# Start of a fused attention and bottleneck kernel: last input tile in four transfers, statistics chunk by chunk, weight sums between the group steps, and eight idle matrix products

## The chip, the cores and the metric

The kernel runs on one NeuronCore of a Trainium2 chip. The metric is the device time of one launch in microseconds (us). The kernel before takes 3301.49 us (median of 3 runs, 3300.69 to 3302.63).

## The reference, cut to what matters

For eight images of 512 channels and 64 x 64 pixels, float32, two residual layers are computed:

```python
x = x + deform_attention(_gn(x))     # layer 0
x = x + bottleneck(_gn(x))           # layer 1

def _gn(v, G=32, eps=1e-5):          # group norm, groups of 16 channels
    g = v.reshape(B_, G, C_ // G, H_, W_)
    m = jnp.mean(g, axis=(2, 3, 4), keepdims=True)
    s = jnp.var(g, axis=(2, 3, 4), keepdims=True)
    return ((g - m) / jnp.sqrt(s + eps)).reshape(v.shape)

q = jnp.einsum('oc,bchw->bohw', w_q, x)   # first step of layer 0, x is normed
```

The rest of layer 0 samples q at 256 learned points, projects keys and values from the samples, and attends from all 4096 pixels with 8 heads. Layer 1 is a narrow convolution stack. The change touches only the group norm of the first image and the first steps of its q projection.

## The kernel before, in words

**Tiling.** An image lies in SBUF as 128 partitions x 4 channel chunks x 4096 pixels. Pixels are cut into 8 tiles of 512. `x_tile(b, t)` is tile t of image b, 128 x 4 x 512, one megabyte. Two images have room at once.

**Order of the work.** Everything is placed by hand, in program order on each engine (`tc.manual_schedule()`, L1058). Generators yield between steps so that the main loop can interleave them. The program starts with image 0 alone:

1. SyncE's queue loads x of image 0 (`load_x(0)`, L1059, eight transfers, L196), then the q weights into `wbuf` (L1060, L135), then x of image 1, then the key and value weights and small ones.
2. `norm_x` (L198) runs one VectorE `bn_stats` for each tile and chunk, 32 in all (L201). `drain` at L1070 lets all of it be issued before anything else.
3. `norm_q` (L209) begins with `group_stats` (L164): four `bn_aggr` (L169), a small product `gps` that averages the means over the groups (L173), four small VectorE operations (L175 to L179), a second product `gpsb` for the variances (L182), and then `ve` (L184) and a power on GpSimd (L185) that gives one over the deviation. It yields after the aggregates, and again ahead of `gpsb`. Back in `norm_q` it yields once more, then normalises tile 1 on GpSimd and tile 0 on VectorE (L217), one chunk after the other, and makes `shift` (L230).
4. `make_q` (L1044, L1078) runs `project_q` (L233). It multiplies each tile by the q weights with seven half-size products in place of eight, in the manner of Strassen and Winograd. For that it needs four sums of quarters of the weights (`of_weights`, L248: s1, s2, a new w21, s4) and four of the quarters of each tile (`of_tile`, L261: t1, t2, a new x12, a new x21). In the loop at L340 to L342 they are issued in turn: s1, t1, s2, t2, w21, x12. s4 follows during tile 0 (L366). Products of tile 0 go p1 (w11, x11), p2 (w12, x21), p6 (s2, t2), p7 (w21, x12), p5 (s1, t1), p4 (w22, x21), p3 (s4, x22), all at L275. Each has four matmuls, and a float32 matmul appears as two matmul instructions in the profile, so that a product has eight.

For image 1 the weight sums are not made again; for later images they are made inside `project_q`, as for image 0.

Of the kernel before, what the change touches and what calls it, by code (L numbers as in the profile page):

```python
# [8 lines left out]
F32 = mybir.dt.float32  # L9
# [7 lines left out]
P = 128  # L17
B = 8
C = 512
NCC = C // P  # L20
HW = 64
N = HW * HW
TP = 512
NT = N // TP
# [25 lines left out]
def kernel(  # L50
# [15 lines left out]
    nc = tc.nc  # L66
    xs = x.rearrange("b (cc p) n -> b p cc n", p=P)
# [7 lines left out]
    ps_a = ctx.enter_context(tc.tile_pool(name="ps_a", bufs=1, space=PSUM))  # L75
# [6 lines left out]
    wbuf = cpool.tile([P, NCC, TP], F32, name="wbuf")  # L82
# [28 lines left out]
    ident = cpool.tile([P, P], F32, name="ident")  # L111
# [43 lines left out]
    def drain(*gens):  # L155
        for gen in gens:
            for _ in gen:
                pass
# [2 lines left out]
    def new_stats(which, b):  # L161
        return small.tile([P, NCC, NT, 6], F32, tag=f"st{which}", name=f"st{which}_{b}")

    def group_stats(st, which, b):  # L164

        nm = f"{which}_{b}"
        mv = small.tile([P, NCC, 2], F32, tag="mv", name=f"mv{nm}")
        for cc in range(NCC):
            nc.vector.bn_aggr(mv[:, cc, :], st[:, cc].rearrange("p t s -> p (t s)"))  # L169
        mean, var = mv[:, :, 0], mv[:, :, 1]  # L170
        yield None
        gps = ps_mm.tile([P, TP], F32, tag="mm", name=f"gps{nm}")
        nc.tensor.matmul(gps[:, :NCC], cst[:, K_GRP : K_GRP + P], mean, start=True, stop=True)  # L173
        gs = small.tile([P, 2, NCC], F32, tag=f"gs{which}", name=f"gs{nm}")
        nc.vector.tensor_copy(gs[:, 0], gps[:, :NCC])  # L175
        dv = small.tile([P, NCC], F32, tag="dv", name=f"dv{nm}")
        nc.vector.tensor_sub(dv, mean, gs[:, 0])
        nc.vector.tensor_mul(dv, dv, dv)
        nc.vector.tensor_add(dv, dv, var)  # L179
        yield None  # L180
        gps2 = ps_mm.tile([P, TP], F32, tag="mm", name=f"gpsb{nm}")
        nc.tensor.matmul(gps2[:, :NCC], cst[:, K_GRP : K_GRP + P], dv, start=True, stop=True)  # L182
        ve = small.tile([P, NCC], F32, tag="ve", name=f"ve{nm}")
        nc.vector.tensor_scalar_add(ve, gps2[:, :NCC], EPS)  # L184
        nc.gpsimd.tensor_tensor(gs[:, 1], ve, nhalf, ALU.pow)  # L185
        return gs
# [7 lines left out]
    def load_x(b, order=range(NT), queue=nc.sync):  # L194
        for t in order:
            queue.dma_start(x_tile(b, t), xs[place[b]][:, :, t * TP : (t + 1) * TP])  # L196

    def norm_x(b, st, order=range(NT)):  # L198
        for t in order:
            for cc in range(NCC):  # L200
                nc.vector.bn_stats(st[:, cc, t, :], x_tile(b, t)[:, cc, :])  # L201
                yield None

    def quarters(a):

        h = C // 2
        return [[a[:, 2 * i : 2 * i + 2, h * j : h * (j + 1)] for j in range(2)] for i in range(2)]

    def norm_q(b, st, norms):  # L209

        gs = yield from group_stats(st, 0, b)
        shift = small.tile([P, NCC], F32, tag="shift", name=f"shift_{b}")

        def normalise(t, cc):
            xc, scale = x_tile(b, t)[:, cc, :], gs[:, 1, cc : cc + 1]
            if t < 2:
                (nc.vector, nc.gpsimd)[t].tensor_scalar(  # L217
                    xc, xc, gs[:, 0, cc : cc + 1], scale, ALU.subtract, ALU.mult
                )
            else:  # L220
                nc.scalar.activation(
                    xc, xc, AF.Identity, bias=shift[:, cc : cc + 1], scale=scale
                )

        norms[b] = normalise
        yield None
        for t in (1, 0):
            for cc in range(NCC):
                normalise(t, cc)
        nc.vector.scalar_tensor_tensor(shift, gs[:, 0], -1.0, gs[:, 1], ALU.mult, ALU.mult)  # L230
        yield None

    def project_q(b, normalise, mq, qd, pools, sums, aside=None):  # L233


# [6 lines left out]
        s1, s2, s4, t1, t2_, first = sums  # L242
# [1 line left out]

        (w11, w21), (w12, w22) = quarters(wbuf)
        V = nc.vector

        def of_weights(n):  # L248

            if b == 1:  # L250
                return
            if n == 1:
                V.tensor_add(s1, w21, w22)
            elif n == 2:
                V.tensor_sub(s2, s1, w11)
            elif n == 3:
                V.tensor_sub(w21, w11, w21)
            else:
                V.tensor_sub(s4, w12, s2)

        def of_tile(t, n):  # L261
            (x11, x12), (x21, x22) = quarters(x_tile(b, t))
            if n == 1:
                V.tensor_sub(t1, x12, x11)
            elif n == 2:
                V.tensor_sub(t2_, x22, t1)
            elif n == 3:
                V.tensor_sub(x12, x22, x12)
            else:
                V.tensor_sub(x21, x21, t2_)  # L270

        def product(bank, w, xh):
            for o in range(2):
                for k in range(2):
                    nc.tensor.matmul(  # L275
                        bank[:, o * 2 * P : (o + 1) * 2 * P],
                        w[:, k, o * P : (o + 1) * P],
                        xh[:, k, :],
                        start=(k == 0),
                        stop=(k == 1),  # L280
                    )
            return bank.rearrange("p (o n) -> p o n", o=2)
# [28 lines left out]
        def two_banks(t, n):  # L311
            two = ps_s.tile([P, 2, TP], F32, tag="s", name=f"pq_{b}_{t}_{n}")
            return two[:, 0, :], two[:, 1, :]
# [24 lines left out]
            )  # L338

        for n in range(1, 4):  # L340
            of_weights(n)
            of_tile(0, n)  # L342
        for t in range(NT):
            (x11, x12), (x21, x22) = quarters(x_tile(b, t))
            (q11, q12), (q21, q22) = quarters(q_tile(b, t))

            def pixels(k):

                if t:
                    by_pixel(t - 1, k)  # L350
                if t + 2 < NT:
                    normalise(t + 2, k)

            bank1, bank2 = two_banks(t, 0)
            p1 = product(bank1, w11, x11)
            p2 = product(bank2, w12, x21)
            nc.scalar.copy(q11, p1)
            of_tile(t, 4)
            if t:
                activate(t - 1)  # L360
            yield 4
            p6 = product(one_bank(t, 1), s2, t2_)
            pixels(0)
            V.tensor_add(q12, q11, p6)
            V.tensor_add(q11, q11, p2)
            if t == 0:  # L366
                of_weights(4)
            yield 2.5
            bank1, bank2 = two_banks(t, 2)
            p7 = product(bank1, w21, x12)  # L370
            pixels(1)
            V.tensor_add(q22, q12, p7)
            if aside and t in (3, 4):
                largest(2, t - 3)
            yield 2.5
            p5 = product(one_bank(t, 3), s1, t1)
            pixels(2)
            V.tensor_add(q12, q12, p5)
            if t + 1 < NT:
                of_tile(t + 1, 1)  # L380
                of_tile(t + 1, 2)
            yield 2.5
            p4 = product(bank2, w22, x21)
            pixels(3)
            V.tensor_add(q21, q22, p4)
            V.tensor_add(q22, q22, p5)
            if t + 1 < NT:
                of_tile(t + 1, 3)
            yield 2.5
            p3 = product(one_bank(t, 4), s4, x22)  # L390
            V.tensor_add(q12, q12, p3)
            if t == 2 and aside:
                aside()
            elif t + 1 < NT:
                largest(t, 0)
                largest(t, 1)
            yield 2
# [171 lines left out]
    exps, sums = {}, {}  # L569
# [469 lines left out]
    norms = {}  # L1039
# [13 lines left out]
    def room_for_sums(tiles):  # L1053

        places = [tiles[i // 2][:, i % 2, :] for i in range(6)]
        return [p.rearrange("p (k o) -> p k o", k=2) for p in places[:5]] + places[5:]

    with tc.manual_schedule():  # L1058
        load_x(0)  # L1059
        load_wq()  # L1060
        load_x(1)

# [4 lines left out]
                nc.sync.dma_start(wkv[i][j], w[:, 2 * j : 2 * j + 2, i * C : (i + 1) * C])  # L1067
        load_weights_late()
        st = new_stats(0, 0)
        drain(norm_x(0, st))  # L1070

        shared = [wout[:, i, :].rearrange("p (k o) -> p k o", k=2) for i in range(3)]
        shared += [kt[:, 0:2, :], kt[:, 2:4, :], wout[:, 3, :]]
        drain(norm_q(0, st, norms))

        st = new_stats(0, 1)
        blocks, other = norm_x(1, st), norm_q(1, st, norms)
# [19 lines left out]
        for g in range(len(names) + LAG):  # L1097
            b, r = divmod(g, ROUNDS)
# [78 lines left out]
    with tc.If(large > 0):  # L1177
        with tc.For_i(0, B, 1) as i:
            b = "m"
# [95 lines left out]
```

## Time and profile before

| quantity | us |
|---|---|
| median of three runs | 3301.49 |
| lowest and highest run | 3300.69, 3302.63 |
| the profiled execution, its own time | 3300.22 |
| span of its trace | 3298.4 |
| time outside the span | 1.8 |
| first `bn_stats` of image 0 starts | 7.31 |
| first product of the q projection starts | 33.71 |

The trace runs from the first to the last instruction of the profiled execution. All later moments are counted in microseconds from the start of the span. A row of the timeline has the start, the length from the first start to the last end, the engine, the line, the operation, the tile written and the tile read, the shapes, the count, and in brackets the idle time of the engine before it with what ended it. PE is TensorE, PEld is its weight load, DVE is VectorE, POOL is GpSimd, ACT is ScalarE and SP is SyncE.

### The profile page before, as it was taken

What the parts mean: (1) busy time and instruction counts of PE and PEld (TensorE: products, weight loads), DVE (VectorE), ACT (ScalarE), POOL (GpSimd) and SP (SyncE); (2) the same over time, 40 slices, a digit from 0 to 9 for tenths busy, and PEclk for the clock granted to TensorE, in tenths of its full rate; (3) what the DMA queues carried; (4) which work ended last, traced back from release to release, by engine and by line L of the source; (5) the groups of instructions that cost most, each with busy time, mean ns of one, the idle gap of its engine ahead of it and who ended that gap; (6) DMA issues with size and microseconds to landing.
All of it is one profiled execution on the core that took longest, in us unless ns stands there. A gap on an engine that the chain in (4) does not pass through costs nothing.

```text
span 3298.4 us, 46059 instructions
## 1 busy us (share of the span) xinstructions
PE 3212.1 (97%) x18196; PEld 1532.3 (46%) x18196; DVE 2321.9 (70%) x3666; ACT 1187.9 (36%) x1641; POOL 606.2 (18%) x576
## 2 busy tenths in 40 slices
PE   6999999999999999999999999999999999999996
PEld 5884223258332583326732276332853338433222
DVE  7885765786757767587766876668766687756565
ACT  2343333344324433344333443335433344333420
POOL 1130300230402204022130312204021040310201
PEclk9999999999999999999999999999999999999996
DMA  7232222662327532284323833257232482322713
GB/s 275 77 99 73 81 69 87 202 134 78 116 77 224 122 90 91 96 224 113 111 85 132 197 91 105 79 188 171 71 97 89 179 179 65 122 71 71 135 38 131
DMA packets 293873, 390.61 MB, mean 118 GB/s; under 512 B 18320, under 2 KB 157840, under 8 KB 293648
## 3 DMA queue, kind: packets, MB, share of 16 engines
q1 hardware_dynamic: 240368, 261.72, 24.3%
q0 software_dynamic: 53280, 125.86, 17.3%
q8 instruction: 145, 2.38, 0.3%
q14 instruction: 80, 0.66, 0.1%
HBM read 193.52 MB, written 192.94 MB: 117 GB/s over the span
## 4 chain that ended last, share of the span: by engine, by line
PE 90%; DVE 6%; issue 2%; DMA 1%; SPq 0%; ACT 0%; POOL 0%; ACTq 0%; DVEq 0%; POOLq 0%
PE pp L666 25%; PE pq L275 24%; PE ps L579 13%; PE pa L597 12%; PE pqt L324 4%; PE pn L624 3%; PE py L749 2%; PE pk L532 2%; PE pv L559 2%; DVE rn L637 1%; PE po L892 1%; DVE st L201 1%; DMA rn<-rn 1%; DVE es L609 1%; DVE rb L650 1%
## 5 line engine op out<-in xcount | busy, mean ns | idle before, releaser
L666 PE MATMUL pp<-image,wout 128*64 128x512 f32 x3584 | 823.5, 602 | 4.9 <-DVE image L652 3.2
L587 ACT ACTIVATE es<-ps 128x1024 f32<-128x1024 f32 x512 | 505.3, 1023 | 289.3 <-PE ps L579 201.3
L666 PEld LDWEIGHTS pp<-image,wout 128*64 128x64 f32 x3584 | 238.0, 137 | 551.8 <-issue 465.5
L597 PE MATMUL pa<-es,vt 128*64 128x512 f32 x2048 | 488.3, 597 | 1.7 <-ACT es L587 1.7
L275 PE MATMUL pq<-image,wbuf 128*128 128x256 f32 x2048 | 476.2, 381 | 1.9 <-DVE image L217 1.9
L518 POOL DMA_INDIRECT g<-qd,row x256 | 274.2, 1071 | 1024.5 <-DVE row L474 842.1
L673 DVE SCALAR_TENSOR_TENSOR image<-pp,vec,image 128x512 f32<-128x512 f32 x224 | 166.8, 745 | 415.4 <-PE pp L666 383.1
L579 PE MATMUL ps<-image,kt 64*64 64x512 f32 x3584 | 442.6, 602 | 1.0
L275 PEld LDWEIGHTS pq<-image,wbuf 128*128 128x128 f32 x2048 | 381.8, 191 | 54.4 <-issue 5.0
L604 ACT COPY image<-pa 128x512 f32<-128x512 f32 x224 | 132.1, 590 | 683.7 <-PE pa L597 628.3
L609 DVE TENSOR_TENSOR es<-es,es 128x1024 f32<-128x1024 f32 x256 | 310.6, 1213 | 71.5 <-PE pa L597 71.4
L597 PEld LDWEIGHTS pa<-es,vt 128*64 128x64 f32 x2048 | 137.3, 136 | 298.0 <-issue 273.9
L579 PEld LDWEIGHTS ps<-image,kt 64*64 64x64 f32 x3584 | 115.5, 132 | 312.1 <-issue 184.6
L637 DVE RECIPROCAL rn<-pn 128x512 f32<-128x512 f32 x64 | 214.7, 3355 | 13.7 <-PE pn L624 6.9
L334 ACT COPY qr<-pqt 128x512 f32<-128x512 f32 x224 | 131.2, 586 | 237.2 <-PE pqt L324 222.2
L185 POOL TENSOR_TENSOR gs<-ve,nhalf 128x4 f32<-128x4 f32 x16 | 16.7, 1042 | 1063.3 <-DVE ve L184 1063.3
L650 DVE STREAM_SHUFFLE rb<-rn 128x512 f32<-128x512 f32 x256 | 187.4, 732 | 0.5 <-issue 0.4
L275 PE MATMUL pq<-es,es 128*128 128x256 f32 x768 | 181.5, 379 | 0.0
L944 POOL DMA_DIRECT2D out_dram<-part x126 | 138.0, 1324 | 161.0 <-ACT part L939 153.7
L201 DVE BATCH_NORM_STATS2 st<-image 128x6 f32<-128x512 f32 x256 | 158.6, 678 | 7.5 <-DMA image<-in_x_dram 7.4
L676 DVE BATCH_NORM_STATS2 st<-image 128x6 f32<-128x512 f32 x224 | 155.6, 695 | 7.7
L652 DVE TENSOR_TENSOR image<-image,rb 128x512 f32<-128x512 f32 x224 | 155.2, 693 | 7.8
(197 smaller groups left out, 3470.2 us busy)
## 6 DMA issues: line engine op xcount, KB each, us to landing
qd<-qr SPq DMA_DIRECT2D x256, 256.0 KB
image<-in_x_dram SPq DMA_DIRECT2D x112, 512.0 KB
out_dram<-image SPq DMA_DIRECT2D x49, 1024.0 KB
image<-in_x_dram POOLq DMA_DIRECT2D x48, 1024.0 KB
out_dram<-part POOLq DMA_DIRECT2D x126, 256.0 KB
image<-in_x_dram SPq DMA_DIRECT2D x16, 1024.0 KB
wbuf<-in_w_kvT_dram SPq DMA_DIRECT2D x14, 1024.0 KB
out_dram<-spare POOLq DMA_DIRECT2D x56, 256.0 KB
```

Source lines behind the costliest of these rows:

```text
L201: nc.vector.bn_stats(st[:, cc, t, :], x_tile(b, t)[:, cc, :])
L275: nc.tensor.matmul(bank[:, o * 2 * P : (o + 1) * 2 * P], w[:, k, o * P : (o + 1) * P], xh[:, k, :], start=(k == 0), stop=(k == 1),)
L518: nc.gpsimd.indirect_dma_start(held[-1][:, i, :, :].rearrange("p j d -> p (j d)"), None, qd[:, :], bass.IndirectOffsetOnAxis(ap=row[:, ky, ...
L579: nc.tensor.matmul(ps[k : k + DH, a, :], kt[r : r + DH, hp, kc * P + k : kc * P + k + DH], qt[r : r + DH, hp, :], start=True, stop=True,)
L587: nc.scalar.activation(e, ps, AF.Exp)
L597: nc.tensor.matmul(pa[a * DH : (a + 1) * DH, :], vt[:, kc, hd * DH : (hd + 1) * DH], es[kc][:, a, :], start=(kc == 0), stop=(kc == 1),)
L609: nc.vector.tensor_add(es[0], es[0], es[1])
L637: nc.vector.reciprocal(rn, denominators.pop((b, t)))
L650: nc.vector.stream_shuffle(rb, rn, [2 * (hp % 2) + hp // 2] * 32)
L666: nc.tensor.matmul(pp[r : r + DH, :], wout[:, hp, oc * P + r : oc * P + r + DH], ao[:, hp, :], start=(hp == 0), stop=(hp == NCC - 1),)
L673: nc.vector.scalar_tensor_tensor(xt[:, oc, :], pp, col(V_BOUT + oc), xt[:, oc, :], ALU.add, ALU.add)
L676: nc.vector.bn_stats(st[:, oc, t, :], xt[:, oc, :])
```

## The change

Six edits, all at the start of the program:

- Tile 7 of image 0 is loaded in four transfers of one chunk each (256 KB) in place of one of 1 MB, on the same queue and in the same place.
- The statistics of tiles 0 to 6 are issued as before. Those of tile 7 are issued inside `group_stats`: statistics of chunk 0, aggregate of chunk 0, statistics of chunk 1, and so on.
- `of_weights` leaves `project_q` for a function of its own. For image 0, s1 is issued ahead of `gpsb`, s2 after the power, and w21 and s4 after the normalising of tiles 1 and 0 and ahead of `project_q`. Images 2 to 7 do as before.
- A new function `keep_up` issues products of the identity with chunk 0 of tile 6, 128 x 128 by 128 x 512, into a PSUM tile that nobody reads.
- Five of them stand ahead of `gps` on TensorE.
- Three of them stand between `gps` and `gpsb`.

```diff
+    def group_stats(st, which, b, last=None):
...
         for cc in range(NCC):
+            if last:
+                last(cc)
             nc.vector.bn_aggr(mv[:, cc, :], st[:, cc].rearrange("p t s -> p (t s)"))
...
+    def of_weights(n, sums):
+        s1, s2, s4 = sums[:3]
+        (w11, w21), (w12, w22) = quarters(wbuf)
+        if n == 1:
+            nc.vector.tensor_add(s1, w21, w22)
+        elif n == 2:
+            nc.vector.tensor_sub(s2, s1, w11)
+        elif n == 3:
+            nc.vector.tensor_sub(w21, w11, w21)
+        else:
+            nc.vector.tensor_sub(s4, w12, s2)
...
         for n in range(1, 4):
-            of_weights(n)
+            if b not in (0, 1):
+                of_weights(n, sums)
             of_tile(0, n)
...
-            if t == 0:
-                of_weights(4)
+            if t == 0 and b not in (0, 1):
+                of_weights(4, sums)
...
+    def keep_up(out, xt, n):
+        for _ in range(n):
+            nc.tensor.matmul(out, ident, xt[:, 0, :], start=True, stop=True)
+
     with tc.manual_schedule():
-        load_x(0)
+        load_x(0, range(NT - 1))
+        for cc in range(NCC):
+            nc.sync.dma_start(x_tile(0, NT - 1)[:, cc, :], xs[0][:, cc, (NT - 1) * TP :])
         load_wq()
...
-        drain(norm_x(0, st))
+        drain(norm_x(0, st, range(NT - 1)))
...
-        drain(norm_q(0, st, norms))
+        last = norm_x(0, st, (NT - 1,))
+        steps = norm_q(0, st, norms, lambda cc: next(last))
+
+        idle = ps_a.tile([P, TP], F32, tag="pa", name="idle")
+        keep_up(idle, x_tile(0, NT - 2), 5)
+        next(steps)
+        next(steps)
+        of_weights(1, shared)
+        keep_up(idle, x_tile(0, NT - 2), 3)
+        next(steps)
+        of_weights(2, shared)
+        drain(steps)
+        of_weights(3, shared)
+        of_weights(4, shared)
```

More of the change, by code (lines that the diff above doesn't have):

```diff
@@ L162, in new_stats @@
         return small.tile([P, NCC, NT, 6], F32, tag=f"st{which}", name=f"st{which}_{b}")
-    def group_stats(st, which, b):
+    def group_stats(st, which, b, last=None):
         nm = f"{which}_{b}"
@@ L207, in quarters, with norm_q @@
         return [[a[:, 2 * i : 2 * i + 2, h * j : h * (j + 1)] for j in range(2)] for i in range(2)]
-    def norm_q(b, st, norms):
-        gs = yield from group_stats(st, 0, b)
+    def norm_q(b, st, norms, last=None):
+        gs = yield from group_stats(st, 0, b, last)
         shift = small.tile([P, NCC], F32, tag="shift", name=f"shift_{b}")
@@ L246, in project_q @@
         V = nc.vector
[L248 to L259, printed above, removed]
         def of_tile(t, n):
```

## The prediction

> **What bounds the kernel now.** I read the page's first lines, then the chain of waits of the first 150 us, then the timeline from 23 to 39 us, row by row. From the page and the chain (start, length, what):
>
> ```profile
> span 3298.4 us, 46059 instructions
> PE 90%; DVE 6%; issue 2%; DMA 1%; SPq 0%; ACT 0%; POOL 0%; ACTq 0%; DVEq 0%; POOLq 0%
> ...
> 1.31 30.69 issue
> 32.05 1.03 POOL gs L185
> 33.11 0.56 DVE image L217
> 33.71 19.17 PE pq L275 x80
> ```
>
> TensorE is the bound: 90% of the whole chain. All that this change touches lies ahead of it: from 33.71 us on the chain is products with no gap until after 140 us. So one number decides, by how much the products of tile 0 start and run earlier or later. The timeline shows what they wait for:
>
> ```profile
> 23.54 2.47 DVE L201 BATCH_NORM_STATS2 st<-image 128x6 f32<-128x512 f32 x4 [0.24 <-DMA image<-in_x_dram]
> 26.25 2.47 DVE L201 BATCH_NORM_STATS2 st<-image 128x6 f32<-128x512 f32 x4 [0.24 <-DMA image<-in_x_dram]
> 28.64 1.04 DVE L169 BATCH_NORM_AGGREGATE mv<-st 128x2 f32<-128x48 f32 x4
> 29.74 0.59 PE L173 MATMUL gps<-mv,cst 128*128 128x4 f32 x2 [29.74 <-DVE mv L169]
> 30.37 0.16 DVE L175 COPY gs<-gps 128x4 f32<-128x4 f32 x1 [0.68 <-PE gps L173]
> ...
> 31.17 0.59 PE L182 MATMUL gpsb<-dv,cst 128*128 128x4 f32 x2 [0.84 <-DVE dv L179]
> 31.80 0.16 DVE L184 TENSOR_SCALAR ve<-gpsb 128x4 f32<-128x4 f32 x1 [0.68 <-PE gpsb L182]
> 32.05 1.02 POOL L185 TENSOR_TENSOR gs<-ve,nhalf 128x4 f32<-128x4 f32 x1 [30.73 <-DVE ve L184]
> 33.11 2.71 DVE L217 TENSOR_SCALAR image<-image,gs 128x512 f32<-128x512 f32 x4 [1.14 <-POOL gs L185]
> ...
> 38.02 0.68 DVE L266 TENSOR_TENSOR kt<-image,kt 128x512 f32<-128x512 f32 x1
> ...
> 38.90 0.38 PE L275 MATMUL pq<-kt,wout 128*128 128x256 f32 x1
> ```
>
> The reader is to see two things. Before tile 7's statistics VectorE idled only 0.24 us: it is nearly as late as the transfers. And p6, whose first matmul starts at 38.90, waited both for TensorE (p1 and p2) and for t2, which VectorE ends at 38.02 + 0.68 = 38.70.
>
> [...] p1 and p2's matmuls start 0.43 us apart at first and 0.22 apart after 37.07. The stretch before the end of the kernel is cold from 3238.07 to 3242.18. The two changes lie 3205.11 us apart, 939 windows of 3.413. So cold stretches of 3.4 and 4.1 us are both seen. [...] `bn_stats` last 0.69 but start 0.60 apart, while L175 to L179, each reading what the one ahead wrote, start 0.03 to 0.04 after its end.
>
> **The change, part by part.**
>
> *Four transfers, and statistics chunk by chunk.* Tiles land 2.71 us apart (statistics that waited for them start at 20.83, 23.54, 26.25), so the chunks of tile 7 should land near 24.2, 24.9, 25.6 and 26.25. VectorE is busy with tile 6 until then: four starts 0.60 apart from 23.54 leave it free at 25.95. So statistics gain 0.30, not two microseconds; the data was never much ahead of VectorE, and four statistics and four aggregates must follow 25.95 in any order. Now each aggregate reads what the instruction just ahead of it wrote, eight in alternation: 0.69 + 0.04 to the aggregate, then 0.32 - 0.08 to the next statistics, 0.97 a chunk. The end is 25.95 + 3 x 0.97 + 0.73 + 0.32 = 29.91, against 28.64 + 1.04 = 29.68. **+0.23**, and -0.27 if dependence costs nothing (29.41), +0.5 if the stall is 0.1 larger a chunk. Transfers: SyncE ended the issue of tile 7 at 14.72 for data that lands at 26.25, so three more issues of about 0.43 (the first tile's) hide in 11 us. The weights move with them on that queue. They should land one megabyte after tile 7, near 28.96, and s1 asks for them near 31.1: 2.1 us of cover, and VectorE's whole queue behind s1 if that were gone.
>
> *Five products ahead.* They wait for tile 6, at 23.5. The nearest row is L559, 128x128 by 128x512 in float32: 16 instructions take 7.13 us, 0.59 the last, so 0.436 a start; a product is two, and twice that cold. Ten instructions take 4.3 us plus half of the cold stretch: with 3.4 to 4.1 us cold, 6.0 to 6.3, to 29.5 to 29.9. That is just ahead of `gps` at 29.97: **0**. If the window falls badly (6.8 us cold) they end at 31.3: +1.3.
>
> *Three products behind.* They sit in TensorE's queue between `gps` and `gpsb`. `gpsb` was 1.43 us after `gps`. Three products are six instructions of 0.43 warm, 2.6 us, and begin some 0.35 after `gps`. So `gpsb` starts 2.9 after `gps`, and `ve`, 0.4 later as warm (end of the kernel: `gps` at 3234.45, its copy at 3234.85), comes 3.3 after it. Before it was 31.80 - 29.74 = 2.06. **+1.26**; nothing hides it, since `ve`, the power, all normalising and p1 stand behind. If still cold they take 5.1: +4.1.
>
> *Sums of weights.* s1 (0.68) runs on VectorE while `gpsb` is out, s2 (0.68, or 1.09 as L264 beside GpSimd) during the power, where VectorE idled 1.14: 0. w21 and s4 now stand ahead of t1 and t2. Ahead of t2's end there were s1, t1 and s2 after `shift`; now there are w21, s4 and t1. The same four operations, so t2 still ends 38.70 - 33.11 = 5.59 after the start of normalising. **0**. That x12 comes one place earlier and s4 is gone from tile 0 is worth nothing, as the products from p6 on run without a gap.
>
> *Warm products.* With TensorE warm, p1 and p2 take 3.5 us plus what they wait for the last chunk, so they end before t2. p6 then waits for t2 alone, at 38.75 instead of 38.90: **-0.15**. Most of what the cold products cost was already hidden behind VectorE. I assume that about 2 us idle around `gpsb` doesn't cool it; if it does, this is 0 or worse.
>
> Sum for the profiled execution: 0.23 + 0 + 1.26 + 0 - 0.15 = +1.34 us, from 3300.22 (3298.4 span, 1.8 outside) to 3301.6. The profiled run lies 1.27 below the median shown; part of that may be a worse phase of the window (up to 1.7 before, up to 1.3 after), which weighs alike on both, so I set the sum on the median: 3301.49 + 1.34 = 3302.8.
>
> **Rivals.** *A, the forecast*: VectorE holds the head, `gpsb` waits: 3302.8. *B, it does its work*: for it speaks that TensorE idled all through the head and was cold; if aggregates do not stall (-0.27), three products fit in the 1.43 us (0), and a typical run of before was colder than the profiled one (-0.15 and some -0.5), the time is 3301.49 - 0.9 = 3300.6. L559's 0.436 a start speaks against it. *C, the idle products stay cold*: [...] No run here shows how plain products with the identity count. Then ten instructions of 0.86 end at 32.1, `gps` 2.4 late; three products take 5.1, +4.1; and p1 and p2 may stay cold to the end (16 x 0.43, up to +1.6): 3301.49 + 6.5 + 0.9 = 3308.9, slower. It decides once `ve` comes over 5 us after `gps`. Against it: L275's plain products warmed in 3.4 us. *D, nothing is added*: the first two terms cancel and the third is hidden somewhere I do not see: 3301.5.
>
> **How the numbers follow.** A 0.70, B 0.13, C 0.06, D 0.11. The time is A's. The range reaches to B and to A with a late window and longer stalls (+1.3 and +0.5, and a run's scatter of 1): 3300.6 to 3305.3. A measurement of this kernel tells some 0.2%, 6.6 us, from no change. A, B and D lie within it; C is slower by 0.22%. Faster 0.01, same 0.94, slower 0.05.
>
> **What would show it.** Right: the last aggregate ends near 29.9; idle products start near 23.5, first 0.86 apart, then 0.43; `ve` comes 3.3 us after `gps`; normalising starts near 34.6; p1's matmuls are 0.22 apart where they do not wait; p6 starts right behind t2, near 40.3. Wrong: an aggregate that ends before 29.4, three products of under 1.5 us, products of tile 0 that wait for something after p6, or a difference beyond 150 us.

## The result, and the profile after

| | us |
|---|---|
| before, median of 18 runs (lowest, highest) | 3300.04 (3294.82, 3304.20) |
| after, median of 18 runs (lowest, highest) | 3306.72 (3300.51, 3310.83) |
| ratio after to before, 95% interval | 1.0017 (1.0010 to 1.0024) |
| the profiled execution of after, its own time | 3308.12 |
| span of its trace | 3306.3 |

The changed kernel is slower by 0.17%; the means of the two sets of runs differ by 5.9 us (standard error 0.9). That is below the 0.2% that the prediction called no change, and above its range, which ended at 3305.3. The forecast was +1.3 us.

From the page of the changed kernel, its first line and the chain's shares by engine:

```profile
span 3306.3 us, 46095 instructions
...
PE 91%; DVE 6%; issue 2%; ACT 1%; DMA 0%; SPq 0%; POOL 0%; ACTq 0%; DVEq 0%; POOLq 0%
```

The bound is what it was. The chain of waits of the first 150 us (start, length, what) shows the head:

```profile
1.31 32.17 issue
33.52 1.41 POOL gs L187
34.95 2.71 DVE image L219 x4
37.73 0.60 DVE wbuf L245
38.33 1.01 DVE wout L247
39.34 0.61 DVE kt L267
39.98 0.70 DVE kt L269
40.72 14.08 PE pq L278 x64
```

In the kernel before the chain went from normalising straight to the 80 matmuls of p1, p2, p6 and on. Now it stays on VectorE until t2 (L269), and TensorE takes over at p6, at 40.72. p6 started at 38.90 before: **the head is 1.82 us later**, of which 0.11 is that the first tile landed later in this execution (first statistics at 7.42, not 7.31).

The timeline from 23 to 43 us shows the steps:

```profile
23.66 3.06 DVE L203 BATCH_NORM_STATS2 st<-image 128x6 f32<-128x512 f32 x5 [0.22 <-DMA image<-in_x_dram]
...
23.77 6.47 PE L1064 MATMUL idle<-image,ident 128*128 128x512 f32 x10 [23.77 <-DMA image<-in_x_dram]
...
28.96 0.64 DVE L203 BATCH_NORM_STATS2 st<-image 128x6 f32<-128x512 f32 x1
...
29.63 0.37 DVE L171 BATCH_NORM_AGGREGATE mv<-st 128x2 f32<-128x48 f32 x1
...
30.07 0.37 PE L175 MATMUL gps<-mv,cst 128*128 128x4 f32 x2
...
30.30 2.82 PE L1064 MATMUL idle<-image,ident 128*128 128x512 f32 x6
...
32.96 0.28 PE L184 MATMUL gpsb<-dv,cst 128*128 128x4 f32 x2
...
33.28 0.16 DVE L186 TENSOR_SCALAR ve<-gpsb 128x4 f32<-128x4 f32 x1 [1.45 <-PE gpsb L184]
33.35 0.68 DVE L243 TENSOR_TENSOR wout<-wout,wbuf 128x512 f32<-128x512 f32 x1
33.52 1.40 POOL L187 TENSOR_TENSOR gs<-ve,nhalf 128x4 f32<-128x4 f32 x1 [32.21 <-DVE ve L186]
34.95 2.71 DVE L219 TENSOR_SCALAR image<-image,gs 128x512 f32<-128x512 f32 x4 [0.92 <-POOL gs L187]
...
35.55 4.12 PE L278 MATMUL pq<-image,wbuf 128*128 128x256 f32 x16 [2.31 <-DVE image L219]
...
39.98 0.69 DVE L269 TENSOR_TENSOR kt<-image,kt 128x512 f32<-128x512 f32 x1
...
40.72 1.99 PE L278 MATMUL pq<-kt,wout 128*128 128x256 f32 x8 [1.05 <-DVE kt L269]
```

The reader is to see three things. `gpsb` stands right behind six idle matmuls, and VectorE idles 1.45 us for it where it idled 0.68. The power at L187 takes 1.40 us, not 1.02, with s2 (L243) running beside it. And p6's bracket says that TensorE now idles 1.05 us for t2: p6 no longer waits for the products ahead of it, whose sixteen matmuls take 4.12 us; in the kernel before they took 5.36, 0.43 us apart until 37.06 and 0.22 after.

The head is the smaller part of the loss, though. Of the 7.9 us between the two spans some 6 arise after p6. So the experiments ask two things: which edit costs what in the head, and what comes after it.

### The profile page after: what moved, and what is told of

The parts are those of the page before. It is cut to its first block, busy times and chain, and to the rows that moved or that the text cites. A ratio compares the mean times of both kernels' runs of the same rounds, so it can differ in the third digit from the quotient of the medians.

```text
span 3306.3 us, 46095 instructions
## 1 busy us (share of the span) xinstructions
PE 3222.4 (97%) x18212; PEld 1535.8 (46%) x18212; DVE 2321.8 (70%) x3666; ACT 1188.2 (36%) x1641; POOL 604.9 (18%) x576
## 4 chain that ended last, share of the span: by engine, by line
PE 91%; DVE 6%; issue 2%; ACT 1%; DMA 0%; SPq 0%; POOL 0%; ACTq 0%; DVEq 0%; POOLq 0%
PE pp L670 26%; PE pq L278 23%; PE ps L583 13%; PE pa L601 12%; PE pqt L327 4%; PE pn L628 3%; PE pk L536 2%; PE py L753 2%; PE pv L563 2%; DVE rn L641 1%; PE po L896 1%; DVE st L203 1%; DVE es L613 1%; PE po L428 0%; DVE rb L654 0%
## 5 line engine op out<-in xcount | busy, mean ns | idle before, releaser
L187 POOL TENSOR_TENSOR gs<-ve,nhalf 128x4 f32<-128x4 f32 x16 | 17.0, 1065 | 1072.3 <-DVE ve L186 1072.3
```

## The experiments

The runs went in five groups on four chips, and chips differ (the kernel before has medians from 3293.7 to 3314.0), so each kernel is compared only with runs of the kernel before in its own group. Where "the chip with the least scatter" is named, it is the one of the first eight rows: the runs of one kernel have a standard deviation of about 1.3 us there, and of 2 to 5 us elsewhere. Differences of means with one standard error are worked out from the runs. The expectations speak of these theories: **H**, the head alone (p6's delay is the whole cost); **L**, something later costs too; **P**, the head's delay moves the later work against the windows of TensorE's clock (in the trace of before all 14 changes of the granted clock, from 37.06 to 3286.55, lie on one grid of 3.413 us; a window is one step of it); **S**, scatter. "p6" is the start of the first p6 matmul in the one profiled execution.

| kernel | before, after (medians) | ratio (95%) | difference of means | p6 |
|---|---|---|---|---|
| same_before | 3294.53, 3294.34 | 0.9999 (0.9991 to 1.0008) | -0.3 | 40.07 |
| stats_only | 3294.53, 3295.04 | 1.0003 (0.9995 to 1.0012) | +0.9 ± 0.4 | 39.17 |
| three_only | 3294.53, 3296.93 | 1.0008 (1.0002 to 1.0015) | +2.8 ± 0.3 | 41.77 |
| no_three | 3294.53, 3294.38 | 1.0001 (0.9993 to 1.0010) | +0.3 ± 0.4 | 39.70 |
| after_again | 3293.71, 3297.77 | 1.0012 (1.0006 to 1.0019) | +3.9 ± 0.3 | 41.00 |
| five_only | 3293.71, 3293.60 | 0.9999 (0.9990 to 1.0007) | +0.2 ± 0.4 | 39.67 |
| sums_only | 3293.71, 3294.76 | 1.0002 (0.9993 to 1.0010) | +0.5 ± 0.5 | 39.38 |
| fitted | 3293.71, 3293.97 | 0.9999 (0.9991 to 1.0008) | +0.3 ± 0.3 | 37.49 |
| plus_two | 3312.76, 3312.76 | 1.0000 (0.9990 to 1.0009) | -1.2 ± 1.3 | 39.76 |
| plus_four | 3312.76, 3311.80 | 0.9996 (0.9985 to 1.0007) | -1.6 ± 1.4 | 38.90 |
| five_behind | 3312.76, 3320.82 | 1.0024 (1.0014 to 1.0035) | +6.5 ± 1.3 | 42.54 |
| fitted_three | 3312.76, 3315.58 | 1.0007 (0.9997 to 1.0017) | +0.8 ± 1.3 | 39.52 |
| after_third | 3301.14, 3307.00 | 1.0018 (1.0010 to 1.0025) | +5.7 ± 1.0 | 41.26 |
| after_filled | 3301.14, 3307.68 | 1.0019 (1.0012 to 1.0026) | +5.6 ± 1.0 | 40.58 |
| before_filled | 3301.14, 3302.61 | 1.0009 (0.9999 to 1.0018) | +2.1 ± 1.1 | 39.81 |
| fitted_filled | 3301.14, 3304.36 | 1.0008 (1.0001 to 1.0015) | +3.1 ± 0.9 | 37.41 |
| plus_two_b | 3313.95, 3315.34 | 1.0006 (0.9998 to 1.0015) | +1.1 ± 1.4 | 38.71 |
| five_behind_b | 3313.95, 3319.79 | 1.0023 (1.0012 to 1.0033) | +7.5 ± 1.4 | 43.39 |

### The kernel before once more

No edit.

> The kernel before, unchanged, as a yardstick: how far apart two profiled executions of one kernel lie, and where. Theory H (head): the change costs what its first 41 us show (p6 starts 1.8 us later), and all that differs beyond is scatter of single half-clock windows of TensorE, each about 1.7 us, that fall at other places in each execution. Then this run's trace has the head of before (p6 within 38.7 and 40.6, by the window's phase) but other half-clock windows than before had, 2 to 6 of them, and a time within 3 us of before. Theory L (later): something beyond the head follows from the change. Then this run's trace matches that of before within 0.5 us all the way from 41 us to the end.

The time is the same. The trace shows how much a head varies with nothing changed: statistics, `gps`, `ve` and normalising lie within 0.02 us of the first trace, but the products of tile 0 stayed cold until 39.41, not 37.06, and p6 started at 40.07, not 38.90, later by half as much. In the six traces whose head is that of before (before, same_before, before_filled, plus_two, plus_two_b, plus_four) p6 starts at 38.71 to 40.07, mean 39.36. In the four of the changed head (after, after_again, after_third, after_filled) it starts at 40.58 to 41.26, mean 40.89. So the head costs 1.5 us on average, a little less than the first two traces say.

### One part at a time: statistics

The kernel before with the four transfers and the statistics of tile 7 in turn with the aggregates:

```diff
-        drain(norm_x(0, st))
+        drain(norm_x(0, st, range(NT - 1)))
...
-        drain(norm_q(0, st, norms))
+        last = norm_x(0, st, (NT - 1,))
+        drain(norm_q(0, st, norms, lambda cc: next(last)))
```

> The kernel before with only the four transfers and the statistics chunk by chunk. Theory H: the last aggregate ends near 29.95, 0.2 to 0.3 later than before, p6 starts near 39.2, the time is within 0.5 us of before but for scatter. Theory L, if the transfers or the order of SyncE's queue are what acts later: 3 us or more above before with the head 0.3 later.

The last aggregate ends at 29.95 with first statistics at 7.37, before at 29.68 with 7.31. That is +0.21 net of the landing, where +0.23 was predicted. p6 at 39.17 lies 0.27 behind the first trace. The time, +0.9 ± 0.4, is a little above.

### One part at a time: five products ahead

The kernel before with `keep_up(idle, x_tile(0, NT - 2), 5)` ahead of `gps`.

> The kernel before with only the five idle products ahead of gps. Theory H: they end between 29.7 and 31.4 by the phase of the window, gps starts then (0 to 1.6 later than before), p1 and p2 run warm, and p6 waits for t2, at 5.65 after normalising: p6 between 38.7 and 40.2, the time within 1 us of before. Theory L, if these products are what acts later: 3 us or more above before.

They ended late here: `gps` starts at 31.17 against 29.74, +1.4. Their weight loads start 0.85 us apart up to 29.84 and 0.43 apart from 30.32 on, where in after_again they are 0.43 apart from 28.72 on. Yet p6 starts at 39.67, and the time is even. TensorE was warm by then (the two instructions of `gps` take 0.28 us, not 0.59), and `ve` came 1.55 us after `gps` and not 2.06. From normalising to p6 it takes 5.64 us with p1 and p2 warm; in the first trace 5.79.

### One part at a time: three products behind

The kernel before with `keep_up(idle, x_tile(0, NT - 2), 3)` between `gps` and `gpsb`.

> The kernel before with only the three products between gps and gpsb added. Nothing warms TensorE ahead, so they run cold: six instructions of 0.86, 5.1 us. Theory H: ve comes 6 us after gps in place of 2.06, normalising and p6 start some 4 us later (p6 near 42.7), and the time is 4 us above before. Theory L: 4 us and, if these products act later, 3 more.

The timeline of TensorE in three_only:

```profile
29.77 0.59 PE L173 MATMUL gps<-mv,cst 128*128 128x4 f32 x2 [29.77 <-DVE mv L169]
30.22 4.26 PE L1060 MATMUL idle<-image,ident 128*128 128x512 f32 x6
34.32 0.28 PE L182 MATMUL gpsb<-dv,cst 128*128 128x4 f32 x2
```

Without the five ahead the three are cold for a stretch (weight loads 0.85 us apart up to 32.92, the next 0.54 later and then 0.43) and take 4.26 us (5.1 was expected), so `ve` comes 4.86 after `gps`, not 2.06: +2.80. p6 is 2.4 later than the mean of before and the time 2.8 ± 0.3 longer. Here the head explains the whole.

### One part at a time: the weight sums

The kernel before with the sums between the group steps:

```diff
-        drain(norm_q(0, st, norms))
+        steps = norm_q(0, st, norms)
+        next(steps)
+        next(steps)
+        of_weights(1, shared)
+        next(steps)
+        of_weights(2, shared)
+        drain(steps)
+        of_weights(3, shared)
+        of_weights(4, shared)
```

> The kernel before with only the weight sums moved. Theory H: s2 beside the power lengthens it from 1.02 to 1.40, so normalising starts at 33.5 in place of 33.1; t2 still ends 5.6 after that or, with the 1.09 of s4, 5.7 to 6.0; p1 and p2 are as cold as before, so p6 starts 0.4 later, and the time is 0.4 us above before (0 to 0.8). Theory L, if the earlier sums act later: 3 us or more above before.

The timeline of sums_only around the power:

```profile
31.92 0.16 DVE L186 TENSOR_SCALAR ve<-gpsb 128x4 f32<-128x4 f32 x1
32.00 0.68 DVE L243 TENSOR_TENSOR wout<-wout,wbuf 128x512 f32<-128x512 f32 x1
32.17 1.40 POOL L187 TENSOR_TENSOR gs<-ve,nhalf 128x4 f32<-128x4 f32 x1 [30.86 <-DVE ve L186]
33.60 2.71 DVE L219 TENSOR_SCALAR image<-image,gs 128x512 f32<-128x512 f32 x4 [0.92 <-POOL gs L187]
```

There is no idle product in this kernel, and the power takes 1.40 us. Normalising starts 1.68 after `ve`, in the kernel before 1.31. So **s2 lengthens the power by 0.38**, and all that follows waits. s2 started first: it had 0.51 us left when the power started. s2 itself took the usual 0.68. What slows the power isn't shown. The power takes 1.02 us in all twelve traces where s2 isn't beside it, and 1.39 to 1.45 in the eight where it is.

### The change without its three products

The changed kernel less `keep_up(idle, x_tile(0, NT - 2), 3)`.

> The changed kernel without the three products between gps and gpsb. Theory H: gpsb starts 1.2 to 1.4 us after gps, normalising near 33.9 (1.0 us earlier than in the changed kernel; the power beside s2 keeps its 1.40), p6 near 39.7, so about 1.1 us less than the changed kernel and 0.8 more than before. Theory L, if the three products are not what acts later: the time stays 4 us or more above before.

`gpsb` follows `gps` by 1.12 us and p6 starts at 39.70; the time is +0.3 ± 0.4. So everything else in the change together costs nothing that can be seen, and the three products, beside the five, cost 3.6 ± 0.5 (after_again less no_three), though p6 differs by 1.3 us only.

### The changed kernel once more

No edit to the changed kernel, in the group on which the times of one kernel differ least.

> The changed kernel, unchanged, once more, beside the kernel before on the same chip in many runs. Theory H (head): its first product that waits for t2 (p6) starts between 40.7 and 42 us, by the phase of the window; the kernel before has p6 between 38.9 (its first profile) and 40.6; so the time is 1.6 us above before on the average (1.0 to 2.2), and the 6 us of the first comparison held scatter. Theory L (later): the time is again 4 us or more above before while p6 differs by no more than 2.

+3.9 ± 0.3. The head gives 1.5. **H falls**, and so does S. Something behind 41 us costs another 2.4. The table sets this trace beside that of same_before; both stem from the same chip. Stages are those from p6 to the first `pk` (the key projection of image 0), to the first `pv`, and so on.

| stretch | same_before | after_again |
|---|---|---|
| p6 to first `pk` | 228.71 | 228.95 |
| first `pk` to first `pv` | 9.72 | 11.09 |
| to the second image's `pv` | 247.20 | 247.36 |
| the next six images, together | 2399.91 | 2399.86 |
| to the last `gps` | 303.94 | 304.05 |
| to the end | 63.51 | 64.98 |

Two stretches stand out, by 1.4 and 1.5 us; the six images are equal. The last stretch is no sign of the change: it lies between 62.8 and 65.6 us in all traces, and is 64.8 in stats_only. The one at the keys is: it is 9.72 or 11.1 to 11.3 and nothing between. TensorE in same_before, then in after_again:

```profile
267.45 1.03 PE L424 MATMUL po<-vec,qs 128*128 128x4 f32 x8
268.77 1.99 PE L532 MATMUL pk<-image,es 128*128 128x256 f32 x8 [0.29 <-ACT pos L433]
271.24 5.45 PE L532 MATMUL pk<-image,es 128*128 128x256 f32 x24 [0.47 <-ACT kt L539]
```

```profile
268.62 1.03 PE L428 MATMUL po<-vec,qs 128*128 128x4 f32 x8
269.94 2.90 PE L536 MATMUL pk<-image,es 128*128 128x256 f32 x8 [0.29 <-ACT pos L437]
273.32 5.91 PE L536 MATMUL pk<-image,es 128*128 128x256 f32 x24 [0.47 <-ACT kt L543]
```

The same instructions take 1.99 and 2.90, then 5.45 and 5.91. The busy times by stretch of after_again (from:to, length, then PE, PEld, DVE, ACT and POOL busy, granted clock, DMA share, GB/s):

```profile
262.00:268.00 6.00, 5.77 (x39) 5.00 (x37) 3.35 (x5) 1.70 (x3) 0.00 (x0) 1.00 0.31 88
270.90:274.30 3.40, 2.93 (x7) 1.85 (x6) 2.44 (x3) 0.38 (x1) 0.00 (x0) 0.50 0.89 214
276.00:280.00 4.00, 4.00 (x23) 2.85 (x26) 0.32 (x1) 1.29 (x4) 0.00 (x0) 1.00 0.85 323
```

and of same_before:

```profile
270.90:274.30 3.40, 3.06 (x14) 2.72 (x15) 1.28 (x2) 0.67 (x2) 0.00 (x0) 1.00 0.98 266
```

For 3.41 us TensorE had half its clock in the changed kernel, in the midst of work. This happens in every kernel of the case: one to seven such stretches, nearly all of 3.41 us, between 41 and 3200 us, mostly near ends and beginnings of images, where the work on TensorE is thin for a moment. Before has them at 320.36, 828.95 and 2429.80; the second and third come 149 and 618 times 3.413 us after the first, on the grid named above. The 18 changes of the granted clock in after lie on such a grid too. Near its end before also has two windows at half clock in a row, 6.83 us from 3235.34. Ahead of the stretch at 320.36 TensorE idled 2.99 us. Near 270 the thin moment is the sixteen matmul instructions of four columns (L428), 1.94 us in after_again, and the wait of 0.29 us ahead of the first `pk`. A half-clock stretch began there in all three traces of the unfilled changed kernel, in neither trace of before. Where a window's end fell between 0.24 us ahead of the first `pk` and 1.20 behind it, the next window was at half clock (after, after_again, after_third, five_only, plus_two, plus_four, fitted_three). Where it fell 1.43 to 2.74 behind, it wasn't (the ten other traces without the filler product told of below). That became theory P. Its expectations call the window there idle. It is thin and not idle: TensorE is busy for 5.77 of the 6 us from 262 to 268 in after_again.

### Idle products that fit

The kernel before with the four transfers (statistics first, then all aggregates), four products ahead, s1 and one product ahead of `gpsb`, two products after it, and the other sums left in place:

```diff
-        drain(norm_q(0, st, norms))
+        steps = norm_q(0, st, norms)
+        idle = ps_a.tile([P, TP], F32, tag="pa", name="idle")
+        keep_up(idle, x_tile(0, NT - 2), 4)
+        next(steps)
+        next(steps)
+        w = quarters(wbuf)
+        nc.vector.tensor_add(shared[0], w[0][1], w[1][1])
+        keep_up(idle, x_tile(0, NT - 2), 1)
+        next(steps)
+        keep_up(idle, x_tile(0, NT - 2), 2)
+        drain(steps)
```

> The kernel before with another set of the same tools, cut to the gaps: the four transfers, but all four statistics of tile 7 and then the four aggregates; four idle products ahead, one between gps and gpsb, two behind gpsb; s1 ahead of gpsb; s2, w21 and s4 where they were before, behind t1, t2 and so on. Theory H: the last aggregate ends near 29.4 in place of 29.7, gps waits for it or for the idle products (29.5 to 30.5), gpsb 1.3 after gps, ve 1.7 after gps, normalising from 32.5 to 33.5, p6 5.0 after that, near 37.7 to 38.5, and the time is 1 to 2 us below before. If the idle products hold gps in most executions, it is even with before. Theory L, if any idle products or transfers act later: above before.

The timeline of fitted:

```profile
29.46 0.39 PE L173 MATMUL gps<-mv,cst 128*128 128x4 f32 x2 [0.65 <-DVE mv L169]
...
32.45 2.71 DVE L217 TENSOR_SCALAR image<-image,gs 128x512 f32<-128x512 f32 x4 [1.14 <-POOL gs L185]
...
37.49 1.99 PE L275 MATMUL pq<-kt,wout 128*128 128x256 f32 x8 [0.33 <-DVE kt L266]
```

The head is mended: last aggregate at 29.41, `gps` to `ve` 1.70, the power 1.02, and p6 1.4 us before that of the first trace, 1.9 before the mean. But the time is even, +0.3 ± 0.3: two microseconds are lost again behind 41 us, as in the changed kernel. That speaks against H from the other side. H had left itself a way out, idle products that hold `gps` back in most executions. Of the three traces with these four products ahead (fitted, fitted_three, fitted_filled) they do so in one, by 0.6 us, which isn't enough for 1.9.

The same with three products in place of the one:

> The kernel called fitted with three products in place of one between gps and gpsb: p6 some 1.65 us later (near 39.1). Theory H: 1.65 above fitted, so 1.9 above before. Theory P: the phases move out of the bad ones, so even with fitted and before: -0.3 to +0.8.

+0.8 ± 1.3 in a group where runs of one kernel differ by some 4.5: it tells little apart. p6 was at 39.52; near 268 there was a half-clock stretch, which P had moved away.

### Moving the phase without the head

The kernel before with two or four products on TensorE in tile 2 of the q projection, far behind the head and ahead of the keys:

```diff
+            if b == 0 and t == 2:
+                idle = ps_a.tile([P, TP], F32, tag="pa", name="idle")
+                for _ in range(2):
+                    nc.tensor.matmul(idle, ident, wbuf[:, 0, :], start=True, stop=True)
```

> The kernel before with two idle products (identity by weights, four instructions of 0.43 warm) behind the last product of tile 2 of image 0, where TensorE has no gap: everything later comes 1.71 us later against the window of 3.413. Theory H (head): the time rises by the 1.71 us that the products take. Theory P (phase): in before, the cold first products pull p6 half along with the window, so that only half of all phases occur[...]. Half a window later, they do: the time rises by 1.71 and some 2 more, 3.2 to 4.2, and half-clock windows near 270 us appear.

> The same with four idle products, 3.42 us, one whole window. Theory H: the time rises by 3.42, twice what plus_two costs. Theory P: the phases are those of before again, so it rises by 3.4 and nothing more (2.9 to 3.9): no more than plus_two within 0.7, though it does twice the idle work.

p6 to the first `pk` grew by 1.7 and 3.9, and in both traces the window near 271 was at half clock: as P says for two products, against P for four. The times are -1.2 ± 1.3 and -1.6 ± 1.4: not even the added products are seen in them.

The changed kernel with five products in place of three:

> The changed kernel with five products in place of three between gps and gpsb: p6 comes 1.71 us later. Theory H: 1.7 above the changed kernel, so 5.6 above before if that is at 3.9. Theory P: the later start moves the phases out of those that hit the stretch near 267, which takes back some 2 us: 2.5 to 4.5 above before, no more than the changed kernel.

+6.5 ± 1.3. No half-clock stretch near 270, as P says; but P's time fails, and H's holds within the error. Both were run again on another chip:

> The kernel plus_two once more: before with 1.71 us of idle products behind tile 2 of image 0. Theory H: 1.7 above before. Theory P: 3.2 to 4.2 above before. On a chip with a scatter of 4 us it stays undecided.

> The kernel five_behind once more: the changed kernel with five products in place of three between gps and gpsb. Theory H: 5.6 above before (1.7 above the changed kernel's 3.9). Theory P: 2.5 to 4.5 above before. On a chip with a scatter of 4 us it stays undecided.

+1.1 ± 1.4 and +7.5 ± 1.4. The trace of plus_two_b has no half-clock stretch near 270, against P; that of five_behind_b has none, as P says. Over both groups two added products cost 0.0 ± 1.0 where P wanted 3.2 to 4.2, and five behind cost 7.0 ± 0.9 where it wanted 2.5 to 4.5. **That the phase decides whether the window near 270 is lost is seen in 17 traces; which kernels lose it P foresaw only in part, and as the account of the time P falls.** More idle products behind cost more, by more than the head shows: p6 in the two traces of five behind is 3.6 us later than the mean of before.

### Filling the thin moment

One product ahead of the first `pk`, in the changed kernel, the kernel before and fitted:

```diff
         next(samples[1])
+        filler = ps_s.tile([P, 2, TP], F32, tag="s", name="filler")
+        nc.tensor.matmul(filler[:, 0, :], ident, wkv[0][0][:, 0, :], start=True, stop=True)
         load_wout()
```

> The changed kernel once more, as the yardstick of the next two on this chip. Theory H (head alone): 1.5 above before (1.0 to 2.2). Theory P (the head moves p6 against TensorE's window, so that the idle window near 267 us, which before hardly has, falls in most executions): 3 to 5 above before, with a half-clock window near 270 us in its trace. Theory S (only scatter between chips and executions): no more than H beyond the interval.

> The changed kernel with one idle product more, between the small offset products of image 1 and the key projection of image 0 (about 267 us), so that the window there is not idle. It costs up to 0.86 us, less the 0.29 that TensorE idles there. Theory H: 0.6 above the changed kernel. Theory P: no half-clock window near 270 us; the stage from the first key product to the first value product takes 9.7 us and not 11.1, so the time is 0.8 us or more below the changed kernel, 1.5 to 3 above before.

> The kernel before with the same one product. Theories H and P alike: 0.6 above before (0 to 0.9), since before has no half-clock window there to lose.

> The kernel called fitted with the same one product. Its head had p6 at 37.5, 1.4 to 2.6 us ahead of before, yet its time was even with before. Theory P: that gain went into the window near 270 us in many executions; filled, it keeps it: 0.3 to 1.5 us below before. Theory H: 0.6 above fitted, so 0.6 to 0.9 above before.

TensorE in after_filled:

```profile
269.11 1.10 PE L1117 MATMUL filler<-es,ident 128*128 128x512 f32 x2
270.05 1.89 PE L536 MATMUL pk<-image,es 128*128 128x256 f32 x8
```

A window's end fell 0.26 us ahead of this `pk`, at the edge of the range that cost the next window before, and in fitted_filled 0.04 ahead, within it. Both kept the full clock, and the first `pk` to the first `pv` takes 9.62 us in all three filled kernels. The filler itself adds 0.5 to 0.7 ahead of it. In the times nothing came back: +5.6 ± 1.0 with it, +5.7 ± 1.0 without. Less 0.6 for the filler, P wanted 0.8 or more; the error of the difference is about 1.4, so this doesn't decide. The other two came out above what either theory said, before_filled at +2.1 ± 1.1 (0.6 expected) and fitted_filled at +3.1 ± 0.9 (at most 0.9 expected). What the filler removes is shown in two traces; what it is worth is not.

## Why the prediction was wrong, point by point

**The head, step by step.**

| step | predicted | after, trace against trace | other traces |
|---|---|---|---|
| first tile lands | 0 | +0.11 | first statistics at 7.16 to 7.46 in all |
| statistics in turn, last aggregate | +0.23 | +0.21 | stats_only +0.21 |
| five ahead, aggregate to `gps` | 0, up to +1.3 | +0.01 | after_again +0.5, after_third +0.8, five_only +1.4 |
| three behind, `gps` to `ve` | +1.26 | +1.15 | after_again, after_third +1.06 |
| s2 beside the power, `ve` to normalising | 0 | +0.36 | sums_only +0.37 |
| normalising to end of t2 | 0 | +0.13 | sums_only, five_behind +0.13 |
| warm p1 and p2, end of t2 to p6 | -0.15 | -0.15 | after_again -0.14 |
| sum | +1.34 | +1.82 | |

The reasoning held for the two large terms. VectorE was nearly as late as the transfers, so splitting the last one could bring only 0.3 us, and the alternation of dependent operations, 0.96 us a chunk (aggregates at 27.71, 28.67 and 29.63), gave it back. And three products do not fit into a round trip of 1.43 us.

**A term mis-sized: "s2 ... during the power, where VectorE idled 1.14: 0".** An engine's idle time is not free for work if the engine that it waits for slows down beside that work. s2 costs 0.38 us there, with no idle product about. The prediction took from the profile of before that an operation on VectorE can last longer while GpSimd works (L264 at 1.09; L253, L255 and L266 took 0.68 in the same stretch) and applied it to s2's own length only, not to the power that holds the path. In the same way "so t2 still ends 5.59 after the start of normalising" counted operations and not their order: t2 (L269) now follows t1 (L267), whose result it reads, directly, and starts 0.71 after it, while before s2 stood between them and neighbours started 0.60 apart. With these two terms, 0.36 and 0.13, the sum is right for this trace.

**Two smaller readings.** The gain of warm products was -0.15 against this one trace. In the six traces with the head of before p6 starts 0.05 to 1.36 us behind t2, 0.66 on the mean, and in the four of the changed head 0.05 or 0.06, so against a typical run the gain is -0.6. And "I assume that about 2 us idle around `gpsb` doesn't cool it" held in three of these four. In after_third a half-clock stretch begins at 35.95, in no_three at 34.87. It costs after_third nothing, as p6 waits for t2 all the same; in no_three p6 starts 0.47 us behind t2.

**The step that failed: "So one number decides, by how much the products of tile 0 start and run earlier or later."** It took what is behind 41 us as fixed, because it is a chain of products without a gap until after 140 us. On the chip with the least scatter the time rose by 3.9 ± 0.3, in the first comparison by 5.9 ± 0.9 (means) and in another group by 5.7 ± 1.0. The head is 1.5 to 1.8 of it. The prediction named "a difference beyond 150 us" as what would make it wrong, and that is what came.

What stands in its place is known in part. Shown: the granted clock changes on a grid of 3.413 us, which lies differently against the work in the traces (a window ends 0.28 us behind the first `pk` in after and 1.5 behind it in before); a window at half clock costs 1.4 to 1.7 us; the window near 270 was lost in all three traces of the unfilled changed kernel and in neither of before. Shown too: of two changed heads one is later by 1.5 and costs 3.9 to 5.9, the other (fitted) is earlier by 1.9 and gains nothing. Not shown: that this window makes the difference. Moving the phase alone (plus_two, plus_four) lost the window and cost nothing that could be measured, and filling the moment brought nothing back.

Stalls of another kind stand in after's own trace too, but they are no mark of the change. VectorE in the kernel before, in its first trace:

```profile
2463.47 0.75 DVE L673 SCALAR_TENSOR_TENSOR image<-pp,vec,image 128x512 f32<-128x512 f32 x1 [8.75 <-remote]
```

and in the changed kernel:

```profile
864.76 0.75 DVE L677 SCALAR_TENSOR_TENSOR image<-pp,vec,image 128x512 f32<-128x512 f32 x1 [8.66 <-remote]
```

VectorE waits over 8 us for something that the profile calls remote, a release for which it shows no instruction. Both traces have two such waits at this line of the kernel. The image of the one at 864 us takes 402.5 us, not 399.7, with no half-clock stretch in it. Waits put down to remote, on VectorE or ScalarE, the longest of 7.6 to 8.8 us, stand in none of the eight traces from the chip with the least scatter and in all twelve others, with the kernel before among them. So they are a likely reason for the larger scatter elsewhere, and none for the +3.9 of after_again.

One more witness is on record for every run and not only for the traced ones: the granted clock over the whole span, to three places. The clock that a run lost is its span times one less that share. On the chip with the least scatter the 21 runs of after_again lost 33.4 us on the mean and the 48 of before 30.9, so 2.5 ± 0.4 us more, and fitted lost 1.7 ± 0.3 us more. That is about what the head leaves open in these two, 2.4 and 2.1. It doesn't settle the cost. no_three and five_only lost 2.1 ± 0.6 and 1.5 ± 0.4 us more and are even in time (part of this can lie in the head, as the stretch of no_three at 34.87 does), and among the 97 runs of before on this chip a microsecond more of lost clock goes with only 0.31 ± 0.07 us of time, a figure that the rounding to three places makes too low.

**Open is the cause of 2 to 4 us** of the loss: each kernel has one trace, and where half-clock stretches fall differs from trace to trace by as much as is sought. The excess is seen where idle products stood both ahead of `gps` and behind it (the changed kernel, five behind, fitted), and not in stats_only, five_only, three_only, sums_only or no_three; fitted_three is too uncertain to place. This is a grouping of the runs and no mechanism.

**The rivals.** B (it does its work) needed aggregates that do not stall and three products that fit in 1.43 us; both are refuted by the timeline. Its third term, that a typical run of before is colder than the profiled one, came true (0.66 us against 0.20 from t2 to p6). C (the idle products stay cold) is refuted: ten idle matmuls took 6.47 us in all and six behind 2.82, and the granted clock is full from 27.67 on, so identity products as plain matmuls do warm the clock here. C's other number, 3308.9 (its 0.9 for p1 and p2 stands without working), was nearer to the result than the forecast, for another reason. D (nothing is added) is refuted by no_three against after_again. The range failed because it was made of the head's terms alone; a bound for the rest was missing, although the prediction itself knew two half-clock stretches in the kernel before.

**What would mend the head** is known: fitted has the head 1.4 us earlier than before in its trace. As a kernel it is even with before, and none of the versions tried is faster.

## What to carry to other kernels

Before you fill a wait with work "for free", look at both sides of it: a filler ahead of a needed instruction on the same engine must end before that instruction is ready (three products of 0.86 us don't fit in 1.43 us: `dv` was ready at 31.23 and `gpsb`, behind them, started at 32.96), and a filler on the idle engine must not slow the engine that it waits for (the power went from 1.02 to 1.40 us). Splitting the last transfer can help by as much as the consumer idles ahead of it, here 0.24 us. A head of 35 us is not the only thing that such a change moves: where the effect is a microsecond or two, work late in the kernel that meets a window at half clock, 1.4 to 1.7 us each, weighs as much, so the range must hold that too, and the sign comes from timed comparisons on one chip, not from one trace.

## What had not been expected of the hardware

- TensorE's clock falls to half for single windows of 3.41 us in the middle of the kernel, one to seven times in an execution between 41 and 3200 us; where one could be set against the same stage without it, it cost 1.4 us (first `pk` to first `pv`, 11.09 us in after_again and 9.72 in same_before) to 1.7 us (sixteen matmuls of L666 in before, 5.35 us from 827.78 and 3.65 from 852.01). In after_again, near 270, the window ahead of the half-clock one held sixteen matmul instructions of four columns, a wait of 0.29 us and less than half of a window of larger products. How little work it takes isn't shown. With one product of 128x512 in it the clock stayed whole in fitted_filled, and in after_filled at the edge of the range.
- The first warm-up differs from one execution to the next of the same kernel: p1 and p2 warmed after 3.35 us in one trace of before and after 5.70 in another, and p6 moved by 1.17 us with it.
- A power on four elements on GpSimd takes 1.02 us alone and 1.40 beside a sum of two 128x512 tiles on VectorE.
- The kernel before has medians from 3293.7 to 3314.0 us on the chips used here, and runs of one kernel have a standard deviation of 1.3 us on one of them and of some 4.5 on another. Waits of about 8 us for something outside the profile, seen in none of the eight traces from the first and in all twelve others, go with it. The same change of 4 us is plain on the first and takes dozens of runs on the other.
